# Second half of the gate/up weights: from one step of four loads to four steps of one load, with a newly searched order of all steps

## The chip, the cores and the metric

The kernel runs on one core of one Trainium2 chip. A time is the device time of one execution in microseconds (us). Three runs of the kernel before gave 573.64, 573.01 and 571.33 us, median 573.01. One more execution was taken with the profiler; it is the source of all durations below.

The engines are called by their names or by the short names of the profile: TensorE (PE, with its weight loads PEld), VectorE (DVE), ScalarE (ACT), GpSimd (POOL) and SyncE (SP). SP computes nothing here; it issues all plain transfers. GpSimd issues the gathers.

## The reference

Four sequences of 512 tokens, 256 features. Each goes through attention (16 heads of 16, causal, with a bias that falls with distance), a residual and a layernorm, and then through a mixture of 64 experts of which each token takes 8, with a shared expert beside them, a residual and a second layernorm:

```python
q, k, v = x @ Wq, x @ Wk, x @ Wv                       # (4, 512, 256), 16 heads
w = softmax((where(causal, q @ k.T, NEG) + slope * (j - i)) / sqrt(16))
x = layernorm(x + (w @ v) @ Wo + bo)
topv, topi = top_k(x @ gate_w.T, 8);  rw = softmax(topv)
gate, up = split(einsum('nh,eih->nei', x, gu_w))       # 64 experts, 64 + 64 wide
out = einsum('nei,ehi->nh', silu(gate) * up * W, dp_w) # W: rw at the chosen experts, else 0
out = out + sigmoid(x @ sh_gate1_w.T) * shared_expert(x)
return layernorm(x + out)
```

The kernel doesn't compute every expert for every token. It sorts the tokens of an expert into slots, runs each expert on its slots alone, writes the results to a table in DRAM (`rows_out`) and gathers for each token the eight rows that belong to it.

## The kernel before, in words

**Strands and letters.** The work is written as twelve generators ("strands"), each of which yields after a step. The string `ORDER` has one letter for each step, 851 in all; the loop at the end of the kernel takes the letters one after the other and advances the strand of that letter by one step. Every engine runs its instructions in the order in which the steps emit them, and so does SP's queue of transfers. Nothing is reordered at run time: the string alone decides what stands behind what. It was found by a search that is not part of the kernel. The strands:

- `p` project: transposes a batch and computes its q, k and v (lines 600 to 634)
- `s` scores: q times k on TensorE (L653), the exponential on ScalarE (L658), the causal mask on GpSimd (L663)
- `v` context: probabilities times v (L681), the transpose and division (L694 to L706), and at the end of a batch the output projection `po` (L715) and the sum with x (L719)
- `r` route: first layernorm, gate logits, the top 8, the slots (`code`), the rows to gather (`at`) and the weights `w8`; its `pick` products run on VectorE (L808) and GpSimd (L811), and its reductions on VectorE (L813)
- `t` turn: closes the memory of the attention and opens the pool `late` in its place
- `h` prepare: splits x into three bf16 parts, builds the one-hot tile `hot`, and runs the second layer of the shared expert (`sd`, L849, L854)
- `g` gather: for a group of 16 experts, brings the tokens into slots by matmuls with `hot` (`px`, L879); ScalarE and VectorE copy the result to `xt` (L869). Two letters a tile, four tiles a group: six matmuls a letter
- `u` up: two letters for a group of four experts ("quad"). The first issues the load of the quad's down weights `dq` (L897, 256 KB, three buffers), the second runs the gate/up matmuls (`gu`, L907) and the activation `ma` (ACT L914, DVE L915, L916)
- `d` down: the down matmuls (`y`, L927), ScalarE's copy `yq` (L932, two buffers), and the transfer of the rows to `rows_out` (L934, SP)
- `i` fetch: one gather of 128 rows from `rows_out` (L945, GpSimd), with five buffers `got`; a batch has 32 of them, and they need all rows of the batch
- `c` combine: VectorE adds a gathered tile with its weight to x (L956); after every 16 of them the second layernorm and the transfer of the output (L963)
- `z` check_range: a flag that tells whether the numbers kept within the range of this path; each engine then loads the flag into a register (L987), which its last branch uses

**Order of the batches.** The attention of the four batches comes first, with routing and slots of earlier batches among it. Then come 16 quads for each batch, and the gathers and combines of a batch among the quads of the next. What remains after the last quad is the gathers and combines of the last batch.

**The gate/up weights.** They are 8 MB, in eight chunks of 1 MB (`gu_sb`, tags `gu0` to `gu7`). One chunk serves two quads, so that quad q reads chunk q // 2, in every batch. Chunks 0 to 3 are loaded at the start of the kernel into memory of their own. Chunks 4 to 7 lie in the pool `late`, in memory that the attention has used. They can only be loaded when its last instruction, the output projection of batch 3, is done. The helper that loads them (L493) is

```python
for c in part:
    g_t = pool.tile([P, GUC, KC, 2, P], FP, tag=f"gu{c}", name=f"gu_sb{c}")
    nc.sync.dma_start(out=g_t, in_=gu[:, c * GUC : (c + 1) * GUC])
    gu_sb.append(g_t)
```

The `dq` buffers lie in the same pool.

Of the kernel before, what the change touches and what calls it, by code (L numbers as in the profile page):

```python
# [28 lines left out]
PRB = (2, 1, 1)  # L29

ORDER = (
    "pppppsppspsvsvsvsppvspppvvvsvsvvsvpspsvvvsvpsvvsvvrrsrpvvvsvsrhsrvrvvsrvssrrrrprvvsvhhhphpsprgsvhvgv"
    "rvsvrsvhhgsvgvrvvrvsvsrvsvvrpprsprsgvrrsrvvsvsgvvvhvrrsprpvrsgvsgrpvsrvpvrvrrsvsvsvvvrsvrssrvrrvsvsv"
    "rrrvvvvvvrvtrugugguuduggruuggrdgruugdugugrduurdguguduuggdggrgdgugguuuggdghuuhrhdhhuuhgduhuhdggudgugr"
    "uuggdgugdruggudgurrudguiirrhuuiiggdgccuguiridggicicucrudgiiguuciduggudcigciciccugurdgcgcucudgiguiiug"
    "gghhdhuuhduggghhudghhcuuduhgcduucuiggdguicugiidccigcdiuguciciuucciggduccigcugiidigccciiuguidciggciuu"
    "ggdcicicugugcccdiuugducuiciggggcgiggcghcdhuudichuuhiicidcihccuciuduuiccgghcgduuhhdgiuugiiidcicuggcud"
    "uggudccicigcdcigicuuuuccgcgiiidcigccucguiidiguuccicducugcdiugcugdgicciguiiuggcidcgiucgcuccidiuiudici"
    "guucccigdgiguiudcicciiugcgugidcidccuuccuiucdiciuuccdciiuidcihcicdicrczczcciicciiiiicccccccicicicicic"
    "iiiiciciciciciciciccccicicicicicicicicicciciccccccc"  # L40
)


# [360 lines left out]
def kernel(  # L404
# [26 lines left out]
    NP = NE // 2  # L431
    GUC = 4
# [21 lines left out]
    def single(name):  # L454
        return ps_s.tile([P, S], FP, tag="s", name=name)
# [34 lines left out]
    def load_gu(pool, part):  # L490
# [4 lines that stand above are left out]
# [61 lines left out]
    def transpose_in(src, b, what, pool, tag, bufs=1):  # L556

        dst = pool.tile([P, KC, S], FP, tag=tag, name=f"{what}_{b}", bufs=bufs)
        for c in range(KC):
            pt = single(f"pt_{what}_{b}_{c}")  # L560
            for t in range(NT):
                nc.tensor.transpose(pt[:, t * P : (t + 1) * P], src[:, t, c * P : (c + 1) * P], ident)
            if c:
                nc.vector.tensor_copy(dst[:, c, :], pt)
            else:
                nc.scalar.copy(dst[:, c, :], pt)  # L566
        return dst
# [29 lines left out]
    qTs, kTs, cxs, probs, late = {}, {}, {}, {}, {}  # L597

    def project():

        for b in range(B):
            xb = xs[b]
            xT = transpose_in(xb, b, "xT", apool, "xT", 2)
            nc.gpsimd.tensor_tensor(xb, xb, bo_b[:, None, :].to_broadcast([P, NT, E]), ALU.add)
            yield
            qT = qTs[b] = apool.tile([P, KC, 2, S], FP, tag="qT", name=f"qT_{b}", bufs=2)
            kT = kTs[b] = apool.tile([P, KC, S], FP, tag="kT", name=f"kT_{b}", bufs=2)
            for c in range(KC):
                for n in "qk":
                    ps = single(f"p{n}_{b}_{c}")  # L610
                    for kc in range(KC):
                        nc.tensor.matmul(  # L612
                            ps, w_sb[n][:, kc, c * P : (c + 1) * P], xT[:, kc, :],
                            start=(kc == 0), stop=(kc == KC - 1),
                        )
                    if n == "k":
                        nc.scalar.copy(kT[:, c, :], ps)
                    else:
                        for par in range(2):
                            nc.vector.tensor_scalar(qT[:, c, par, :], ps, own[:, par : par + 1], None, ALU.mult)  # L620
                    yield
            for t in range(0, NT, 2):
                pv = single(f"pv_{b}_{t}").rearrange("p (t h d) -> p t h d", h=HEADS, d=HD)
                for u in range(2):
                    for kc in range(KC):
                        nc.tensor.matmul(  # L626
                            pv[:, u], xT[:, kc, (t + u) * P : (t + u + 1) * P], w_sb["v"][:, kc, :],
                            start=(kc == 0), stop=(kc == KC - 1),
                        )
                for u in range(2):  # L630
                    nc.vector.tensor_tensor(
                        vas[b % 2][:, t + u, :, 0:HD], pv[:, u],
                        decay[:, t + u, :, None].to_broadcast([P, HEADS, HD]), ALU.mult,
                    )
                yield
# [5 lines left out]
    def scores():  # L641

        for b in range(B):
            for c, par, n in units:
                widths = [S - kb * P for kb in blocks[n]]
                pr = apool.tile([P, 4, sum(widths)], FP, tag=f"pr{n}", name=f"pr_{b}_{c}_{par}_{n}", bufs=PRB[n])
                probs[b, c, par, n] = pr
                s_ps = [double(f"sT_{b}_{c}_{par}_{n}_{i}") for i in range(2)]
                for m, kb in enumerate(blocks[n]):
                    lo = sum(widths[:m])  # L650
                    for r in range(4):
                        rows = slice(32 * r, 32 * r + 32)
                        nc.tensor.matmul(  # L653
                            s_ps[r // 2][:, r % 2, lo : lo + widths[m]], kTs[b][rows, c, kb * P : (kb + 1) * P],
                            qTs[b][rows, c, par, kb * P :], start=True, stop=True, skip_group_check=True,
                        )
                for i in range(2):
                    nc.scalar.activation(  # L658
                        pr[:, 2 * i : 2 * i + 2, :], s_ps[i][:, :, : sum(widths)], AF.Exp, scale=1.0 / HD**0.5
                    )  # L660
                for m in range(len(widths)):
                    lo = sum(widths[:m])
                    nc.gpsimd.affine_select(  # L663
                        out=pr[:, :, lo : lo + P], in_=pr[:, :, lo : lo + P], pattern=[[0, 4], [1, P]],
                        compare_op=ALU.is_ge, fill=0.0, base=0, channel_multiplier=-1,
                    )
                yield
# [157 lines left out]
    def prepare():  # L825

        for b in range(B):
            parts[b] = [mpool.tile([P, NT, E], BF, tag=f"x{n}", name=f"x{n}_{b}") for n in "hml"]
            for t in range(NT):
                h, m, l = (p[:, t, :] for p in parts[b][:3])  # L830
                xb = xs[b][:, t, :]
                left = mpool.tile([P, E], FP, tag="left", name=f"left_{b}_{t}")
                nc.scalar.copy(h, xb)
                nc.vector.tensor_tensor(left, xb, h, ALU.subtract)
                nc.scalar.copy(m, left)
                nc.vector.tensor_tensor(l, left, m, ALU.subtract)
                yield
                o = mpool.tile([P, WIDTH, NE], BF, tag=f"hot{t}", name=f"hot_{b}_{t}")
                nc.vector.tensor_tensor(
                    o, codes[b][:, t, None, :].to_broadcast([P, WIDTH, NE]), window, ALU.is_equal  # L840
                )
                parts[b].append(o)
                yield

            sa, sig = shares[b]
            sd = double(f"sd_{b}").rearrange("p j (t e) -> p (j t) e", e=E)
            for t in (0, 2, 1, 3):
                i = t // 2
                nc.tensor.matmul(  # L849
                    sd[:, t, :], sa[64 * i : 64 * i + 64, (t % 2) * P : (t % 2 + 1) * P],  # L850
                    shdp_sb[64 * i : 64 * i + 64, :], start=True, stop=True,
                )
            for t in range(NT):
                nc.vector.scalar_tensor_tensor(  # L854
                    xs[b][:, t, :], sd[:, t, :], sig[:, t, :], xs[b][:, t, :], ALU.mult, ALU.add
                )
            yield
# [110 lines left out]
    def turn():  # L968

        early.close()  # L970
        late["pool"] = fast.enter_context(tc.tile_pool(name="late", bufs=1))
        load_gu(late["pool"], range(NP // GUC // 2, NP // GUC))
        yield

    def check_range():

# [11 lines left out]
        yield  # L988

    strands = dict(  # L990
        p=project(), s=scores(), v=context(), r=route(), t=turn(), h=prepare(), g=gather(), u=up(), d=down(),
        i=fetch(), c=combine(), z=check_range(),
    )
    with tc.manual_schedule():
# [64 lines left out]
```

## Time and profile before

| what | value |
|---|---|
| median of three runs | 573.01 us |
| profiled execution | 531.3 us |
| its span, first to last instruction | 529.5 us |
| mean granted clock of TensorE | 0.936 |
| TensorE busy | 437.3 us, 83% |
| VectorE busy | 336.6 us, 64% |
| ScalarE busy | 246.1 us, 46% |
| GpSimd busy | 210.3 us, 40% |
| moved by DMA | 82.10 MB, mean 155 GB/s |

The profile is of one execution; this one took 531.3 us, of which 1.8 lie outside the span. A row of the list of instructions gives the start, the length, the engine, the line, the operation with "output <- inputs", the shape, and in brackets how long the engine stood idle before it and what ended this. "SPq" is SP issuing a transfer: the length is that of issuing, not of moving data. In the table of stretches a row gives the stretch, its length, the busy time of PE, PEld, DVE, ACT and POOL, the granted clock, the busy share of the DMA engines and GB/s.

### The profile page before, as it was taken

The numbers are of one execution on the slowest core, as the hardware profiler recorded it, in microseconds if no ns is written. First come the engines' busy times: TensorE is split into PE (matmuls) and PEld (weight loads), VectorE is DVE, ScalarE is ACT, GpSimd is POOL, SyncE is SP. The second block draws the span as 40 slices with busy tenths as digits, with TensorE's granted clock in tenths as the row PEclk, the third lists the DMA queues.
The fourth block names the chain that finished last, engine by engine and source line by source line (L and its number), as shares of the span: only waits on it lengthen the run. The fifth ranks groups of instructions, "written<-read, shape, count | busy, mean of one in ns | idle before, by whom it ended". The sixth has DMA issues, their size and how long they took to land.

```text
span 529.5 us, 12357 instructions
## 1 busy us (share of the span) xinstructions
PE 437.3 (83%) x4873; PEld 298.9 (56%) x4873; DVE 336.6 (64%) x944; ACT 246.1 (46%) x446; POOL 210.3 (40%) x233
## 2 busy tenths in 40 slices
PE   4999999999999986799999999999999899800000
PEld 2545455555446545587877777876778777700000
DVE  2312467786767664364777888778877687765633
ACT  1374657565553751355655556555655455400000
POOL 7051413433233231000004670174564657567770
PEclk9999999999999999799999999999999999975555
DMA  8800000000000006565555886696888889953331
GB/s 245 344 1 1 2 1 1 2 1 1 1 1 1 2 2 256 188 232 181 181 204 195 280 278 229 239 309 213 289 294 277 289 297 318 302 180 111 118 101 33
DMA packets 31907, 82.10 MB, mean 155 GB/s; under 512 B 4704, under 2 KB 10336, under 8 KB 30816
## 3 DMA queue, kind: packets, MB, share of 16 engines
q1 hardware_dynamic: 25696, 64.44, 34.3%
q0 software_dynamic: 6144, 16.79, 10.8%
q8 instruction: 40, 0.66, 0.6%
q14 instruction: 27, 0.22, 0.1%
HBM read 45.55 MB, written 35.65 MB: 153 GB/s over the span
## 4 chain that ended last, share of the span: by engine, by line
PE 51%; DMA 17%; issue 15%; DVE 6%; POOL 5%; ACT 3%; SPq 1%; POOLq 0%; DVEq 0%; ACTq 0%
DMA got<-rows_out,at 13%; PE gu L907 9%; PE sT L653 9%; PE av L681 6%; PE px L879 5%; PE y L927 5%; POOL got L945 5%; PE pq L612 3%; PE pk L612 3%; DMA dq<-in_dp_dram 3%; PE pv L626 3%; PE po L715 3%; ACT pr L658 2%; DVE x L956 2%; PE pt_c L694 2%
## 5 line engine op out<-in xcount | busy, mean ns | idle before, releaser
L945 POOL DMA_INDIRECT got<-rows_out,at x128 | 132.3, 1033 | 152.8 <-DVE x L956 66.1
L907 PE MATMUL gu<-xt,gu_sb 128*64 128x128 f32 x2048 | 125.7, 276 | 0.0
L907 PEld LDWEIGHTS gu<-xt,gu_sb 128*64 128x64 f32 x2048 | 110.9, 137 | 18.5 <-issue 17.1
L658 ACT ACTIVATE pr<-sT 128x768 f32<-128x768 f32 (+1 forms) x96 | 79.1, 881 | 43.2 <-PE sT L653 43.2
L956 DVE SCALAR_TENSOR_TENSOR x<-got,w,x 128x256 f32<-128x256 f32 x128 | 63.0, 494 | 42.1 <-DMA got<-rows_out,at 40.8
L932 ACT COPY yq<-y 128x1024 f32<-128x1024 f32 x64 | 64.8, 1012 | 45.1 <-PE y L927 41.0
L663 POOL TENSOR_SCALAR_AFFINE_SELECT pr<-pr 128x512 f32<-128x512 f32 x64 | 40.9, 651 | 106.4 <-ACT pr L658 105.2
L927 PE MATMUL y<-dq,ma 64*128 64x256 f32 x512 | 69.4, 390 | 10.7 <-DMA dq<-in_dp_dram 9.3
L869 DVE COPY xt<-px 128x512 f32<-128x512 f32 x64 | 43.7, 684 | 25.9 <-ACT xt L869 25.3
L927 PEld LDWEIGHTS y<-dq,ma 64*128 64x128 f32 x512 | 46.1, 189 | 19.6 <-issue 12.4
L869 ACT COPY xt<-px 128x192 f32<-128x192 f32 (+1 forms) x128 | 46.4, 376 | 20.2 <-PE px L879 15.8
L653 PE MATMUL sT<-qT,kT 32*128 32x256 f32 (+3 forms) x512 | 54.0, 467 | 0.3 <-ACT pr L658 0.2
L914 ACT ACTIVATE ma<-gu 128x256 f32<-128x256 f32 x64 | 24.6, 384 | 55.1 <-PE gu L907 55.1
L879 PE MATMUL px<-hot,xh 64*128 64x320 bf16 x256 | 39.6, 303 | 5.3 <-ACT xt L869 3.3
L915 DVE SCALAR_TENSOR_TENSOR ma<-ma,gu 128x256 f32<-128x256 f32 x64 | 26.6, 416 | 22.1 <-ACT ma L914 21.9
L681 PE MATMUL av<-pr,va 128*32 128x128 f32 (+3 forms) x512 | 40.4, 438 | 0.3 <-ACT xT L566 0.3
L879 PE MATMUL px<-hot,xl 64*128 64x320 bf16 x256 | 39.1, 299 | 0.0
L879 PE MATMUL px<-hot,xm 64*128 64x320 bf16 x256 | 39.0, 299 | 0.0
L811 POOL TENSOR_TENSOR pick<-pick,rest 128x512 f32<-128x512 f32 x16 | 20.8, 1302 | 42.1 <-DVE pick L808 35.5
L653 PEld LDWEIGHTS sT<-qT,kT 32*128 32x128 f32 x512 | 25.1, 183 | 18.7 <-issue 12.8
L916 DVE TENSOR_TENSOR ma<-gu,ma 128x256 f32<-128x256 f32 x64 | 27.1, 424 | 2.2
L681 PEld LDWEIGHTS av<-pr,va 128*32 128x32 f32 x512 | 13.7, 109 | 25.8 <-issue 18.1
(116 smaller groups left out, 483.2 us busy)
## 6 DMA issues: line engine op xcount, KB each, us to landing
rows_out<-yq SPq DMA_DIRECT2D x64, 512.0 KB, 4.2
dq<-in_dp_dram SPq DMA_DIRECT2D x64, 256.0 KB, 4.5
gu_sb<-in_gu_dram SPq DMA_DIRECT2D x8, 1024.0 KB, 8.9
x<-in_x_dram SPq DMA_DIRECT2D x4, 512.0 KB, 6.2
got<-rows_out,at POOLq DMA_INDIRECT x128, 3.7
out_dram<-x SPq DMA_DIRECT2D x8, 256.0 KB, 3.3
wq_sb<-in_wq_dram SPq DMA_DIRECT2D x1, 256.0 KB
wk_sb<-in_wk_dram SPq DMA_DIRECT2D x1, 256.0 KB
```

Of the source, the lines that this page charges most:

```text
L612: nc.tensor.matmul(ps, w_sb[n][:, kc, c * P : (c + 1) * P], xT[:, kc, :], start=(kc == 0), stop=(kc == KC - 1),)
L653: nc.tensor.matmul(s_ps[r // 2][:, r % 2, lo : lo + widths[m]], kTs[b][rows, c, kb * P : (kb + 1) * P], qTs[b][rows, c, par, kb * P :], st ...
L658: nc.scalar.activation(pr[:, 2 * i : 2 * i + 2, :], s_ps[i][:, :, : sum(widths)], AF.Exp, scale=1.0 / HD**0.5)
L663: nc.gpsimd.affine_select(out=pr[:, :, lo : lo + P], in_=pr[:, :, lo : lo + P], pattern=[[0, 4], [1, P]], compare_op=ALU.is_ge, fill=0.0, ...
L681: nc.tensor.matmul(av[32 * r : 32 * r + 32, kb * P :], vas[b % 2][:, kb, 8 * c + 2 * r + par, :], pr[:, r, lo : lo + w], start=(kb == 0), ...
L869: copy(xt[:, kc, :, t * CELL + lo : t * CELL + hi], ps[:, kc, lo * GROUP : hi * GROUP].rearrange("p (s e) -> p e s", e=GROUP),)
L879: nc.tensor.matmul(ps[:, kc, first : first + WIDTH * GROUP], parts[b][i][PART * half : PART * half + PART, t, kc * P : (kc + 1) * P], o[PA ...
L907: nc.tensor.matmul(gu_ps[64 * e : 64 * e + 64, j, which, :], gu_sb[p // GUC][:, p % GUC, kc, which, 64 * e : 64 * e + 64], xt[:, kc, QUAD ...
L927: nc.tensor.matmul(ys[:, e, j, :], a[64 * e : 64 * e + 64, j, :], dq[64 * e : 64 * e + 64, j, :], start=True, stop=True,)
L932: nc.scalar.copy(yq.rearrange("s j e h -> s e j h"), ys)
L945: nc.gpsimd.indirect_dma_start(out=g, out_offset=None, in_=rows_out[b], in_offset=bass.IndirectOffsetOnAxis(ap=ats[b][:, t, k : k + 1], ax ...
L956: nc.vector.scalar_tensor_tensor(acc[:, t, :], got.pop(n), w8s[b][:, t, k : k + 1], acc[:, t, :], ALU.mult, ALU.add)
```

## The change

The step `t` no longer loads chunks 4 to 7. A new strand `l` (`rest_of_up`) loads one of them at each of its four steps. The string has four letters more, and all of it is new: another search was run with the new letter, so that nearly every step from the first scores steps on stands at another place. Apart from the places, the same steps are taken: the numbers of `p`, `s`, `v`, `r`, `h`, `g`, `u`, `d`, `i`, `c` and `z` are unchanged.

```diff
@@ ORDER (cut to the lines around the turn) @@
-    "rrrvvvvvvrvtrugugguuduggruuggrdgruugdugugrduurdguguduuggdggrgdgugguuuggdghuuhrhdhhuuhgduhuhdggudgugr"
...
+    "vhrvvvvvrgvrvtgggrruuugguugllldrruguduuggggrgdguuduggurrddguuugudgguluggduggghuhduuhdhhuhugduuggdhud"
...
@@ turn @@
         early.close()
         late["pool"] = fast.enter_context(tc.tile_pool(name="late", bufs=1))
-        load_gu(late["pool"], range(NP // GUC // 2, NP // GUC))
         yield
+
+    def rest_of_up():
+
+        for c in range(NP // GUC // 2, NP // GUC):
+            load_gu(late["pool"], [c])
+            yield
@@ strands @@
-        p=project(), s=scores(), v=context(), r=route(), t=turn(), h=prepare(), g=gather(), u=up(), d=down(),
+        p=project(), s=scores(), v=context(), r=route(), t=turn(), l=rest_of_up(), h=prepare(), g=gather(), u=up(), d=down(),
         i=fetch(), c=combine(), z=check_range(),
```

What SP issues around the turn, in the order of its queue:

| before | after |
|---|---|
| chunk 4, 5, 6, 7 | dq_0, dq_1, dq_2 |
| dq_0, dq_1 | chunk 4, 5, 6 |
| rows_out of y_0 | rows_out of y_0 |
| dq_2, dq_3 | dq_3 |
| rows_out of y_1 | rows_out of y_1 |
| dq_4 ... | dq_4 ..., and chunk 7 between rows_out of y_6 and dq_9 |

Other places that move: the projections of batch 1 (`p`) come together ahead of the first context steps of batch 0. TensorE has six groups of px and two of gu between `po` and y_0, where it had three and two. Before the last down step 94 gathers are issued instead of 93, and the last two gathers of batch 2 and the first one of batch 3 stand ahead of the register load of `z` in GpSimd's queue, where all three stood behind it.

More of the change, by code (lines that the diff above doesn't have):

```diff
@@ L31 @@
 ORDER = (
-    "pppppsppspsvsvsvsppvspppvvvsvsvvsvpspsvvvsvpsvvsvvrrsrpvvvsvsrhsrvrvvsrvssrrrrprvvsvhhhphpsprgsvhvgv"
-    "rvsvrsvhhgsvgvrvvrvsvsrvsvvrpprsprsgvrrsrvvsvsgvvvhvrrsprpvrsgvsgrpvsrvpvrvrrsvsvsvvvrsvrssrvrrvsvsv"
-    "rrrvvvvvvrvtrugugguuduggruuggrdgruugdugugrduurdguguduuggdggrgdgugguuuggdghuuhrhdhhuuhgduhuhdggudgugr"
[L35 to L40, printed above, removed]
+    "pppppsppspsppppsppvvvsvsvsvvspsvvsvvsvspvsvvsvsvsvvrvvsvsrrvsvvvrhsvrrsvvsrhrsvrsprrphprppshvvvvrgpg"
+    "vsvrsvhvpsrvvrrvrsvsvsvvsrsvhhvrsvvsprvsvvhrsrvrsvvgrrpprgvrpsrvgpsvrrrvrsvsvvsvvgrsrrsvvvvrrsrssrrg"
+    "vhrvvvvvrgvrvtgggrruuugguugllldrruguduuggggrgdguuduggurrddguuugudgguluggduggghuhduuhdhhuhugduuggdhud"
+    "gughugugdrgugdruudugguughidriiigdggcruuccgiuiicciigdggruccicuuiidiggcuuiggccrdiguucccdiugudgrgcuuiig"
+    "gcdcugigghhudhuuhdughudghhuuhgduugcgduuiicggdcigcucigiudggciciccuuicggdguuiicdigchcdicuicuiguciuggdc"
+    "cciuiudicccguggucicdcgugiccuiidigiuugdccciggicuiuigggcrgidghcuuhdhhuuduhicchgicucdugigiduhuugghcdugu"
+    "gdgcuugdcicuuicggiccciduiuiccicidgigugcgiucgidcuicgucciidgcuiugdccgcuiiugdcccgiucgicdgicuugudcgcigcu"
+    "iiggiuccciduiuiigccdicugcuccidiguiuicduudcccuciciuducuidiccuiihcidrcciicdiicizzcicicicicccccciiciicc"
+    "iciicicicicicicicciiciccccicicicicicicicicicicicccccccc"
 )
```

## The prediction

> **What bounds the kernel now.** I read the engine totals first, then the slices, then the wait that stands out in them, and last the end of the span. Engine totals and slices of the page of before (a digit is tenths of a slice of 13.2 us):
>
> ```profile
> PE 437.3 (83%) x4873; PEld 298.9 (56%) x4873; DVE 336.6 (64%) x944; ACT 246.1 (46%) x446; POOL 210.3 (40%) x233
> ...
> PE   4999999999999986799999999999999899800000
> ...
> PEclk9999999999999999799999999999999999975555
> DMA  8800000000000006565555886696888889953331
> ```
>
> (In the third line the digits begin right after the name; it is the granted clock of TensorE.) TensorE is full from slice 2 to about slice 35, with one notch at slices 16 and 17, and has nothing to do in the last five. So there are two stretches with different limits: TensorE sets the time up to its last expert step at 465 us, and after that a tail of 64.5 us runs through the gathers of the last batch. A hole in TensorE's line before 465 us is time of the kernel, one for one.
>
> The notch in the list of TensorE's instructions, and what SyncE (SP) issued then (start, length, both us; in brackets the idle time before):
>
> ```profile
> 205.38 1.97 PE L907 MATMUL gu<-xt,gu_sb 128*64 128x128 f32 x32
> 215.29 2.08 PE L927 MATMUL y<-dq,ma 64*128 64x256 f32 x8 [7.95 <-DMA dq<-in_dp_dram]
> ...
> 221.89 1.03 PE L927 MATMUL y<-dq,ma 64*128 64x256 f32 x8
> ```
>
> ```profile
> 202.26 2.07 SPq L493 DMA_DIRECT2D gu_sb<-in_gu_dram  x4
> 204.38 0.97 SPq L897 DMA_DIRECT2D dq<-in_dp_dram  x2
> 218.45 0.33 SPq L934 DMA_DIRECT2D rows_out<-yq  x1
> ```
>
> The first down step y_0 wants its weights dq_0 (256 KB) at 207.3. They were issued at 204.4, behind four 1 MB loads of gate/up weights in the same queue, and came at 215.2: 10.8 us, where the DMA issues give a median of 4.5 us for dq. The stretches around it show why: 430 GB/s from 208 to 212, all engines full, and the clock at 0.58 and 0.56 from 212 to 220.
>
> ```profile
> 208.00:212.00 4.00, 0.00 (x0) 0.00 (x0) 0.66 (x2) 0.00 (x0) 0.00 (x0) 1.00 1.02 430
> 212.00:216.00 4.00, 0.70 (x4) 0.68 (x6) 0.00 (x0) 0.00 (x0) 0.00 (x0) 0.58 0.77 313
> 216.00:220.00 4.00, 4.00 (x36) 2.79 (x34) 1.22 (x3) 1.66 (x3) 0.00 (x0) 0.56 0.20 80
> ```
>
> Start of the tail (GpSimd's list):
>
> ```profile
> 466.99 0.99 POOL L945 DMA_INDIRECT got<-rows_out,at  x1 [0.30 <-DVE w L813]
> 470.42 0.99 POOL L945 DMA_INDIRECT got<-rows_out,at  x1 [2.43 <-DVE x L956]
> 471.71 0.99 POOL L945 DMA_INDIRECT got<-rows_out,at  x1 [0.30 <-issue]
> 473.01 1.00 POOL L945 DMA_INDIRECT got<-rows_out,at  x1 [0.30 <-issue]
> ```
>
> The last 34 gathers run from 470.42 to 515.24 at a pitch of 1.30 us. Counted back from the end, 470.42 and 471.71 belong to batch 2, and 473.01 is the first of batch 3.
>
> **The Trainium skill.** "DMA: Bandwidth & Descriptors", section "Queues, rings and completion order", says that an SDMA engine takes the descriptors of one ring in ring order. The trace agrees: dq_0 came only after the 4.2 MB ahead of it. "TensorE: Matmul & The Clock Gate", Part 1, says that after an idle window of about 3.4 us TensorE runs at half clock until it has been busy about as long. The trace agrees: after 7.95 us of idling y took 2.08 us instead of 1.03.
>
> **The change, part by part.** The same instructions run in both kernels. What changes is the order, which the two instruction lists show.
>
> *Removed: four gate/up loads ahead of dq_0.* SP now issues dq_0, dq_1, dq_2, then three of the loads, and the fourth between dq_8 and dq_9. What goes: 7.95 us of idling, and the slow clock after it: y 2.08 - 1.03 = 1.05; twelve px 1.60 for 0.92 (chain), 0.68; gu 2.16 for 1.90, 0.26. Sum 9.95 us.
>
> *Does the wait go elsewhere?* Count from P, the end of the last output projection po (202.05 in before), when SP is released, as memory of the attention comes free; dq_0 now carries this wait. dq_0 issued at P+0.2 lands at P+4.7 (4.5 median) to P+5.3 (5.1 in this stretch). TensorE has before y_0: six px groups of 0.46, two gu of 1.90: P+6.6. VectorE has before ma_0 (from P+0.9): xt 0.68, w 0.68, three small ones 0.56, statistics 1.76, then ma 0.85: P+5.4. So no wait at y_0, by a margin of 1.2 us.
> Behind it, the three loads: 3 x 1.05 + 3 x 0.26 = 3.93 MB at 430 GB/s are 9.1 us, so from P+1.0 they fill the queue to about P+10. The first rows_out is issued at P+8.9 (y_0 to P+7.6, copy 1.0) and lands at about P+13.5 rather than P+13.1. It holds up yq_2, which is due at P+17: from y_0 to y_2 TensorE has gu 1.9, px 0.5, y 1.0, gu 1.9, px 1.8, transposes 1.0, px 0.5. dq_3, issued after it (SP is in order), lands at about P+14.5; y_3 comes at P+19.5. Nothing waits, with 3.5 us and 5 us in hand. Chunks 4 to 6 are first read by gate/up step 8, chunk 7 by step 14, each over 20 us of TensorE work after its load; the fourth load delays dq_9 and one rows_out by 1.05 MB / 430 GB/s = 2.4 us, with 3 dq buffers and 9 us from issue to use. Cost 0; without this cover 2.4 us.
>
> *Moved: the rest of the order.* Attention: TensorE idles 4.1 us in 10 to 200 (190 less 39.7, 49.5, 49.0, 47.7). In the new order batch 1 is projected right after batch 0. Between a scores step and the context step that reads it lie under 2.5 us of TensorE work in 4 cases (3 before); the exp of 2 x 0.88 and the mask of 0.65 need that. Taken 0, from -2 to +3 us, as no row shows this order.
> Expert steps: I put TensorE's 1.90, 0.96 and 0.46 us on the letters. Between a gather and its combine lie under 3 us in 17 cases of the first 92, before in 10. A gather takes 1.0 and lands 3.7 later, so VectorE waits there, and behind it stand xt copies and ma. In before such waits sum to 17.6 us up to 463 us, and TensorE lost 3.2 us through VectorE (1.7, 0.2, 1.3). Times 17/10: 2.2 us lost. Adjacent px halves (0.41 each) are 7 instead of 8: -0.4. Net +1.8, from 0 to +5.
> Tail: in before, the range check's register load (0.53 us, issued 469.0) stands in GpSimd's queue ahead of the last two gathers of batch 2, which so start 1.4 us after the flag. In the new order these two are ahead, and batch 3's first gather stands ahead of the load. It can start when the last rows_out has landed: last y ends at 464.96, issue 466.13, landing 4.0: 470.1 instead of 473.01. The load then costs 0.5 to 1.4 between the first and second gather; the 0.5 us by which layernorm held up a gather at 480.06 goes. Gain 2.0 to 2.9, taken 2.4.
>
> Sum: -9.95 + 1.8 - 2.4 = -10.55. Of the profiled 531.3 us (span 529.5) 520.7 are left. The median of the runs, 573.01, is 42 us above this execution, and nothing in the profile says where they lie; I take the same microseconds off: 562.4. Scaled by 573/531 it would be 561.6.
>
> **Rivals.** *The wait comes back three steps later* (yq_2 on rows_out, y_3 on dq_3). Against it stand 3.5 and 5 us of margin at 430 GB/s. If the loads ran at only 178 GB/s (what moved from 215 to 260, where nothing pressed), 3.93 MB took 22 us and dq_3 came at P+24.5: 5 us of hole and up to 1.5 us of slow clock. Gain 4: 569.
> *No gain in the runs.* The 42 us would be a limit on TensorE's work over time, and the hole merely rest. Against it: clock 1.00 in nearly all full stretches. 573.
> *Slower: the combines.* Seven more short gaps times up to 2.7 us (4.7 less 2) are 19 us of VectorE standing still between 300 and 465 us. If all of it reached TensorE, 573.0 - 12.35 + 19 = 580. It decides from 15 us on; before passed on 3.2 of 17.6. That speaks against it, but TensorE has only two PSUM buffers for gate/up to run ahead.
> *More gain*: the runs have a longer hole than the profile (slower transfers), worth 16 us: 557 or less.
>
> **How the numbers follow.** Forecast as worked out 0.72 (own range 557 to 567), back later 0.10, no gain 0.05, slower 0.08, more 0.05. 0.5%, about what a measurement of this kernel can tell, is 2.9 us: 570.1 to 575.9. Faster: 0.72 + 0.10 + 0.05 less 0.02 at the edge = 0.85; same 0.07; slower 0.08. The range 555 to 569 leaves out slower and no gain, the upper half of "back later", and the far end of "more": under 0.2.
>
> **What would show it.** Right: no idle over 1 us before the first y, no clock dip near 215, dq_0 landing in about 5 us, last y about 8 us earlier, batch 3's first gather about 5 us after it. Wrong: an idle time at y_3 or yq copies <- rows_out (the return), VectorE's waits for got well over 30 us ahead of the last y with px waiting for xt (the slower rival), or a new idle time over 3 us of TensorE in the attention.

## The result, and the profile after

| runs | before, us (runs) | changed, us (runs) | ratio, 95% interval | difference |
|---|---|---|---|---|
| the comparison that the forecast was made for | 572.33 (4) | 565.60 (4) | 0.9887 [0.9849, 0.9925] | -6.7 us |
| both kernels again, chip A | 572.48 (18) | 566.91 (6) | 0.9911 [0.9887, 0.9935] | -5.6 us |
| both kernels, chip C | 530.54 (11) | 518.03 (5) | 0.9756 [0.9740, 0.9773] | -12.5 us |

One of the 18 runs of before on chip A took 1524 us and is left out of the ratio. The change makes the kernel faster by 1.1%; the forecast was 562.4 us, 1.85% under 573.01. The table also shows where the 42 us lie between the profile of before (531.3 us) and its timed runs (573 us), which the forecast had left open. They go with the chip. The experiments ran on four, called A to D here: before takes 572 us on A and 531.3, 530.5 and 531.7 us on B, C and D. The profile that the forecast read is like B, C and D. The times that it had to forecast are like A, and so is the first profile of the changed kernel, of an execution of 567.88 us. Engine totals and slices of its page (a slice is 14.1 us):

```profile
PE 453.8 (80%) x4873; PEld 308.8 (55%) x4873; DVE 337.2 (60%) x944; ACT 245.5 (43%) x446; POOL 210.1 (37%) x233
...
PE   4999999999999899999879799978997876930000
...
PEclk9999999999999999999998899997999989885555
```

The notch at slices 16 and 17 is gone. But from slice 20 on TensorE has small holes and dips of its clock, and its 4873 matmuls are busy for 16.5 us longer than in the profile of before. On chip C the same kernel shows none of that (a slice is 12.9 us):

```profile
PE 433.7 (84%) x4873; PEld 295.7 (57%) x4873; DVE 340.4 (66%) x944; ACT 246.2 (48%) x446; POOL 209.4 (40%) x233
...
PE   4999999999999999999999999999999998810000
...
PEclk9999999999999999999999999999999999965555
```

TensorE is full from slice 2 to slice 33, with no notch and no dip of the clock before the tail. The mechanism of the forecast is therefore read on chip C, against the profile of before, which is of the same kind. TensorE's instructions around y_0, then SP's (start, length, in us; `...` stands for rows that are cut, here and below):

```profile
204.34 1.97 PE L907 MATMUL gu<-xt,gu_sb 128*64 128x128 f32 x32
...
206.66 1.03 PE L927 MATMUL y<-dq,ma 64*128 64x256 f32 x8
207.62 1.97 PE L907 MATMUL gu<-xt,gu_sb 128*64 128x128 f32 x32
...
209.93 1.03 PE L927 MATMUL y<-dq,ma 64*128 64x256 f32 x8
```

```profile
199.70 1.28 SPq L897 DMA_DIRECT2D dq<-in_dp_dram  x3
201.02 1.38 SPq L493 DMA_DIRECT2D gu_sb<-in_gu_dram  x3
208.78 0.33 SPq L934 DMA_DIRECT2D rows_out<-yq  x1
209.22 0.36 SPq L897 DMA_DIRECT2D dq<-in_dp_dram  x1
```

y_0 starts with no idle time in brackets, 7.1 us after the last output projection (13.2 in before), and takes 1.03 us instead of 2.08. Of the three dq loads, now first in the queue, dq_1 lands 3.0 us after its issue and dq_2 5.7 us; the landing of dq_0 is not on record. dq_3, issued behind the three gate/up loads at 209.2, takes 6.8 us. The table of stretches (columns as before: length, PE, PEld, DVE, ACT, POOL, clock, DMA share, GB/s) shows that the DMA engines are full again, while TensorE works on:

```profile
204.00:208.00 4.00, 4.00 (x60) 3.10 (x57) 3.74 (x13) 1.80 (x5) 0.00 (x0) 1.00 0.94 337
208.00:212.00 4.00, 4.00 (x64) 3.37 (x62) 3.58 (x18) 2.44 (x4) 0.00 (x0) 1.00 1.00 411
212.00:216.00 4.00, 3.53 (x48) 2.61 (x44) 2.79 (x6) 2.02 (x7) 0.00 (x0) 1.00 0.97 383
```

From 208 to 212 they move 411 GB/s and TensorE is busy for all of the 4 us; in before it was busy for 0.00 us of the stretch with 430 GB/s.

The span in three parts, from the instruction lists (P is the end of the last output projection, E the start of the copy of the last y, both in us from the start of the span):

| stretch | before (profile on record) | changed, chip C | difference | forecast |
|---|---|---|---|---|
| start to P | 202.1 | 199.6 | -2.5 | 0 |
| P to E | 263.0 | 254.7 | -8.3 | -9.95 + 1.8 = -8.15 |
| E to the end | 64.4 | 63.2 | -1.2 | -2.4 |
| span | 529.5 | 517.5 | -12.0 | -10.55 |

### The profile page after: what moved, and what is told of

Its sections match the earlier page's. It is cut to its first block, busy times and chain, and to the rows that moved or that the text cites. A ratio compares the mean times of both kernels' runs of the same rounds, so it can differ in the third digit from the quotient of the medians.

```text
span 565.9 us, 12367 instructions
## 1 busy us (share of the span) xinstructions
PE 453.8 (80%) x4873; PEld 308.8 (55%) x4873; DVE 337.2 (60%) x944; ACT 245.5 (43%) x446; POOL 210.1 (37%) x233
## 4 chain that ended last, share of the span: by engine, by line
PE 71%; issue 7%; ACT 6%; another core or an unknown queue 5%; DVE 4%; DMA 4%; POOL 1%; POOLq 0%; SPq 0%; ACTq 0%; DVEq 0%
PE gu L907 21%; PE px L879 11%; PE y L927 10%; PE sT L653 7%; PE av L681 6%; PE pq L612 3%; PE po L715 3%; PE pk L612 3%; PE pv L626 3%; DMA got<-rows_out,at 2%; ACT pr L658 2%; PE pt_c L694 2%; ACT xt L869 2%; PE pl L736 1%
## 5 line engine op out<-in xcount | busy, mean ns | idle before, releaser
L907 PE MATMUL gu<-xt,gu_sb 128*64 128x128 f32 x2048 | 136.2, 286 | 4.0 <-issue 3.9
L907 PEld LDWEIGHTS gu<-xt,gu_sb 128*64 128x64 f32 x2048 | 118.6, 143 | 25.5 <-issue 24.4
L927 PE MATMUL y<-dq,ma 64*128 64x256 f32 x512 | 72.7, 398 | 0.3 <-issue 0.2
L879 PE MATMUL px<-hot,xh 64*128 64x320 bf16 x256 | 40.8, 309 | 28.2 <-ACT xt L869 25.3
L869 ACT COPY xt<-px 128x192 f32<-128x192 f32 (+1 forms) x128 | 46.4, 375 | 26.0 <-PE px L879 17.8
L927 PEld LDWEIGHTS y<-dq,ma 64*128 64x128 f32 x512 | 48.3, 194 | 9.7 <-issue 4.5
L653 PE MATMUL sT<-qT,kT 32*128 32x128 f32 (+3 forms) x512 | 51.8, 467 | 0.5 <-ACT pr L658 0.5
L879 PE MATMUL px<-hot,xl 64*128 64x320 bf16 x256 | 41.0, 305 | 1.5 <-issue 1.5
L879 PE MATMUL px<-hot,xm 64*128 64x320 bf16 x256 | 40.5, 304 | 2.0 <-issue 2.0
L879 PEld LDWEIGHTS <-xh 64*128 64x128 bf16 x256 | 14.5, 95 | 46.1 <-issue 43.8
```

The source lines that it names most:

```text
L653: nc.tensor.matmul(s_ps[r // 2][:, r % 2, lo : lo + widths[m]], kTs[b][rows, c, kb * P : (kb + 1) * P], qTs[b][rows, c, par, kb * P :], st ...
L869: copy(xt[:, kc, :, t * CELL + lo : t * CELL + hi], ps[:, kc, lo * GROUP : hi * GROUP].rearrange("p (s e) -> p e s", e=GROUP),)
L879: nc.tensor.matmul(ps[:, kc, first : first + WIDTH * GROUP], parts[b][i][PART * half : PART * half + PART, t, kc * P : (kc + 1) * P], o[PA ...
L907: nc.tensor.matmul(gu_ps[64 * e : 64 * e + 64, j, which, :], gu_sb[p // GUC][:, p % GUC, kc, which, 64 * e : 64 * e + 64], xt[:, kc, QUAD ...
L927: nc.tensor.matmul(ys[:, e, j, :], a[64 * e : 64 * e + 64, j, :], dq[64 * e : 64 * e + 64, j, :], start=True, stop=True,)
```

## The experiments

All were run beside the kernel before on the same chip. The first four ran on chip B, the next three on C, the next four on A, the last on D.

**The kernel before again.** No edit.

> The kernel before, unchanged, once more with the profiler, since its first profiled execution (531.3 us) was 40 us shorter than its timed runs and the changed kernel's (567.9 us) was not. If the 531.3 us were an exception: about 572 us, with TensorE standing still for 3 to 6 us about ten times after the gathers begin (about 280 us), as in the changed kernel's profile. If the profiler shortens this kernel's execution: about 531 us again. The last output projection po should end near 202 us and the first y should start near 215 us, after about 8 us without its weights, in either case.

531.76 us, and the same timeline: P at 202.5, first copy at 218.4, after 8.6 us in which y_0 waited for dq_0. So the profile on record was no exception among executions, and the profiler doesn't shorten anything: all 34 timed runs of before on chip B lie between 529.0 and 534.2 us.

**The loads alone, in the old order.**

```diff
 source of the changed kernel; ORDER of before, with the letters l put in
-    ...vtrugugguuduggruug...
+    ...vtrugugguudulllggruug...      and the fourth l ahead of the tenth dq load
```

> The old order, with only the four loads moved: three behind the third dq load, the fourth ahead of the tenth. Theory (the hole is the gain, 9.95 us by the forecast's sum): 562 to 563 us, ratio 0.983, no idle time of TensorE ahead of the first y. Rival (the gain comes from the new order of the other steps): 572 us. Rival (loads only shift the wait to the yq copies or a later y): 568 us and an idle time over 2 us at y_2 or y_3.

528.36 us against 531.33 (ratio 0.9936, 0.9917 to 0.9955): -3.0 us, near the third of these (-4 on the scale of 572). y_0 waits for nothing, but y_3 does. TensorE's list, with y_2 and y_3:

```profile
215.29 1.03 PE L927 MATMUL y<-dq,ma 64*128 64x256 f32 x8
...
223.03 2.08 PE L927 MATMUL y<-dq,ma 64*128 64x256 f32 x8 [3.90 <-DMA dq<-in_dp_dram]
```

And SP's:

```profile
201.99 0.80 SPq L897 DMA_DIRECT2D dq<-in_dp_dram  x2
209.22 0.33 SPq L934 DMA_DIRECT2D rows_out<-yq  x1
209.59 0.43 SPq L897 DMA_DIRECT2D dq<-in_dp_dram  x1
210.07 1.80 SPq L493 DMA_DIRECT2D gu_sb<-in_gu_dram  x3
211.99 0.36 SPq L897 DMA_DIRECT2D dq<-in_dp_dram  x1
```

This is the forecast's rival "the wait comes back", at the place that it named. In this order the step d_0 stands ahead of the third dq load. SP is in order, so rows_out of y_0, which waits for the copy of y_0, held dq_2 and the three loads behind it until 209.2. The loads went out at P + 8.2, in the changed kernel at P + 1.5. So dq_3 was issued right behind three of these loads and came 11.0 us later, and the y behind the wait ran at half speed (2.08 us).

**The order alone.** The changed kernel's ORDER without its letters l, and the four loads back in the step t, ahead of dq_0.

```diff
-    ...vtgggrruuugguugllldrr...
+    ...vtgggrruuugguugdrr...          and load_gu(... range(NP // GUC // 2, NP // GUC)) in turn()
```

> The new order of all other steps, but the four loads back in the step t, ahead of dq_0. Theory: the new order gives next to nothing by itself (forecast -0.6), but has 2.6 us more TensorE work ahead of the first y, so a hole of about 6 us and 2 us of slow clock come back: about 8 us over the changed kernel, 573 to 574 us. Rival (the gain comes from the order): 566 us, as the changed kernel.

530.14 us against 531.33 (0.9989, 0.9973 to 1.0005): no difference that can be told. The hole is back:

```profile
213.57 2.08 PE L927 MATMUL y<-dq,ma 64*128 64x256 f32 x8 [7.41 <-DMA dq<-in_dp_dram]
```

So neither part has the gain by itself (-1.2 and -3.0 us; together -12.5 on chip C). The new order does shorten the attention: P comes at 198.9 us here, at 202.5 in before on this chip. But P to E takes 264.9 us instead of 262.8, so most of that is lost again while the hole stands. I had expected 6 us of hole, as TensorE has three more groups of px ahead of y_0; but dq_0, now issued together with two more, came 12.5 us after its issue (at 201.1) instead of 10.8.

**The range check moved back.**

```diff
 from the last d on
-    d iicizzcic ...
+    d zczciiiic ...
```

> The changed kernel with the range check put back ahead of the last two gathers of batch 2 and the first of batch 3, as in the kernel before. Theory (the tail step of the forecast): 2.4 us slower than the changed kernel, about 568 us. Rival (the tail is held by something else, such as the last rows_out or the combines of batch 2): no difference, 565.6 us.

521.12 us on chip B, 0.9799 (0.9770 to 0.9827) of before. Without the changed kernel on the same chip this does not tell what the step is worth; the pair on chip A below does.

**The changed kernel on the same chip as before.** No edit.

> The changed kernel, unchanged, beside the kernel before on the same chip. The runs so far suggest that one chip takes about 531 us for the kernel before (the profiled execution of before, and all experiments so far) and another about 572 us (the timed runs and the profile of the changed kernel). Theory: where before takes 531 us, the changed kernel takes 521 to 522 us, ratio 0.981, as the forecast's sum against the profile had it, and TensorE has none of the dozen stalls of 3 to 6 us. Rival: the gain is 1.1% on every chip, 525.5 us. The tail step of the forecast would make it 2.4 us faster than the kernel with the range check moved back (521.1 us), 518.7 us; from that kernel's profile I now expect no gain there, because the fifth gather after batch 3's first one waits for a got buffer in place of it.

518.03 us, 0.9756 of before: better than the 521 to 522 that I expected. The stalls of the first profile are absent, so the rival of 1.1% on every chip falls. The number lies near what the forecast's tail step asked for here (518.7). That would have been the wrong reason, as the pair on chip A shows.

**Loads one by one, in the old order.**

```diff
-    ...vtrugugguuduggruuggrdgruugdugugrduurd...
+    ...vtrugugguuduggruulggrdgruulgdugulgrduulrd...
```

An l stands behind each letter that issues dq_3, dq_4, dq_5 and dq_6.

> The old order with the four loads placed one by one behind the loads dq_3, dq_4, dq_5 and dq_6, where three in a row behind dq_2 had brought a wait of 3.9 us at y_3. Theory: the hole is the gain and the order of the other steps matters little: no idle time over 1 us up to y_8, 521 to 522 us where before takes 531. Rival (the new order itself is worth several us): 525 us or more.

525.98 us against 530.54 (0.9907, 0.9884 to 0.9929): -4.6 us, the rival's number. y_3 no longer waits for weights. But now each of the next four rows_out stands behind a gate/up load in the queue, and ScalarE's copies, with two yq buffers, wait for rows_out to land. ScalarE's list:

```profile
225.77 1.01 ACT L932 COPY yq<-y 128x1024 f32<-128x1024 f32 x1 [3.09 <-DMA rows_out<-yq]
...
230.13 1.01 ACT L932 COPY yq<-y 128x1024 f32<-128x1024 f32 x1 [2.53 <-DMA rows_out<-yq]
...
234.51 1.01 ACT L932 COPY yq<-y 128x1024 f32<-128x1024 f32 x1 [2.54 <-DMA rows_out<-yq]
```

From P to the copy of y_3 this kernel needs 19.0 us (before 28.3), but from there to y_7 16.5 (before 13.5): 3 of the 9.3 us are given back. Beside the changed kernel its span is 6.6 us longer (524.1 us against 517.5): 2.6 us of that lie ahead of P, 2.4 between P and E, 1.6 in the tail. So when the loads go out one by one, most of what is left lies outside the stretch that the loads touch. Whether the old order would keep the whole gain with the three loads right behind dq_1, ahead of the first rows_out, was not run.

**Eight buffers for gathered rows.**

```diff
-RING = 5
+RING = 8
```

> The changed kernel with eight buffers for gathered rows instead of five. Theory (the tail is held up where the sixth gather of batch 3 waits for a buffer that stands behind batch 2's layernorm on VectorE): this wait of 1.8 us (3.1 us pitch instead of 1.3) and a smaller one of 0.5 us later go, 2 us faster than the changed kernel, about 519.5 us. Rival (the tail is set by 1.3 us a gather and by the last rows_out): the same as the changed kernel.

510.24 us on chip C, 0.9614 (0.9598 to 0.9631) of before and 7.8 us under the changed kernel, where I expected 2. The tail gave 3.0 us (E to the end 60.1 us instead of 63.2), but the larger part came before the last y: P to E took 248.9 us instead of 254.7. GpSimd's list around E (449.5 us):

```profile
447.25 1.00 POOL L945 DMA_INDIRECT got<-rows_out,at  x1 [0.31 <-issue]
448.55 1.00 POOL L945 DMA_INDIRECT got<-rows_out,at  x1 [0.30 <-DVE x L956]
454.72 1.00 POOL L945 DMA_INDIRECT got<-rows_out,at  x1 [5.17 <-DVE x L956]
```

All of batch 2 is gathered before the last y has left PSUM, and batch 3's first gather starts at E + 5.2, 4.2 us after the issue of the last rows_out (450.5). The row names VectorE, but the combine that frees its buffer lay eight gathers back. The likelier releaser is the landing of rows_out, which took 4.0 us in the median of the changed kernel's profile and so falls at about E + 5. TensorE's waits between 200 and 450 us fall to two rows, 3.8 us, with none for VectorE. This is the fastest version that was run.

**The changed kernel and the range check, both on chip A.** Kernels as above.

> The changed kernel again, to have it on one chip with the kernel that has the range check moved back. Where before takes 531 us: 518 us again. Where before takes 572 us: 565.6 us again, with TensorE's signals coming 1 to 6 us late about a dozen times.

> The changed kernel with the range check moved back, again, now on the same chip as the changed kernel. In the two profiles so far the tail itself, counted from the last y, differs by only 0.3 us (63.5 against 63.2), and 2.7 us lie before the last y, where both kernels issue the same instructions. Theory A (the 2.7 us came from the other chip; the range check costs what the tails show): 0.3 us slower than the changed kernel, same. Theory B (the forecast's step: 2.4 us): 2 to 3 us slower than the changed kernel on the same chip too.

566.91 and 566.97 us, ratios to before 0.9911 (0.9887 to 0.9935) and 0.9890 (0.9867 to 0.9914). Theory A holds: moving the range check is worth nothing that can be measured. The 2.7 us that lay before the last y between chips B and C (P to E 257.5 and 254.7 us) were not its doing. So chips that are alike in before can differ by 2 to 3 us in the changed kernel.

**Eight buffers in the kernel before, chip A.**

```diff
-RING = 5
+RING = 8
```

> The kernel before with eight buffers for gathered rows. If the five buffers cost what they cost the changed kernel (7.8 us): about 523 us where before takes 531 us. If the new order is what makes the buffers short: less than 3 us gained, 528 us or more.

575.70 us against 572.48 (1.0067, 1.0038 to 1.0096): slower by 0.7%. Neither of my two numbers covers that, both being worked out from a chip of the other kind. On chip A, letting gathers run ahead brought nothing.

**The kernel before with a profile, chip A.**

> The kernel before, for a profile on the same chip as the changed kernel. About 531 us or about 572 us, as the chip is; in the second case with the late signals of TensorE in it too. Its TensorE idles 7 to 8 us ahead of the first y in either case.

572.05 us. The profiles of chip A show what this document calls late signals: an instruction that waits for TensorE starts some us after TensorE's recorded end. The matmuls are the same, in the same order, on chip A and on chip B. From the list of all engines, chip A:

```profile
361.96 1.97 PE L907 MATMUL gu<-xt,gu_sb 128*64 128x128 f32 x32
...
364.61 1.05 POOL L945 DMA_INDIRECT got<-rows_out,at  x1 [0.30 <-issue]
...
365.10 0.47 PE L927 MATMUL y<-dq,ma 64*128 64x256 f32 x1 [0.45 <-issue]
...
366.50 0.94 PE L927 MATMUL y<-dq,ma 64*128 64x256 f32 x3 [0.93 <-issue]
...
367.26 0.99 POOL L945 DMA_INDIRECT got<-rows_out,at  x1 [0.30 <-issue]
367.94 1.24 PE L927 MATMUL y<-dq,ma 64*128 64x256 f32 x4 [0.50 <-issue]
...
368.56 1.00 POOL L945 DMA_INDIRECT got<-rows_out,at  x1 [0.30 <-issue]
...
370.92 0.38 ACT L914 ACTIVATE ma<-gu 128x256 f32<-128x256 f32 x1 [7.85 <-remote]
```

And chip B:

```profile
351.91 1.97 PE L907 MATMUL gu<-xt,gu_sb 128*64 128x128 f32 x32
...
353.92 0.38 ACT L914 ACTIVATE ma<-gu 128x256 f32<-128x256 f32 x1 [0.91 <-PE gu L907]
...
354.22 1.03 PE L927 MATMUL y<-dq,ma 64*128 64x256 f32 x8
```

On B ma starts 0.04 us after the last matmul of gu has ended, and the eight matmuls of y run in one piece. On A ma starts 7.0 us after it, and y comes in three pieces, each after an idle time that ends with "issue". The waits say it in one row, "ACT ma <- remote" (the profile finds no releaser), which the profiles of B, C and D do not have at all. Chip A, before:

```profile
ACT ma L914 <- remote: 32.4, 7, 7.9
```

For each of the 64 quads, take the time by which ma starts later than both the last gu matmul's end and the end of ScalarE's previous instruction. On A this is over 0.6 us in 18 quads of before, 44.9 us in all, and in 15 and 13 quads of the changed kernel's two profiles of this kind (42.7 and 37.1 us). On B and C it is at most 0.05 us in any quad. On A it goes with the gathers. In before, the 24 quads with no gather issued in the 5.5 us ahead of ma have a mean of 0.03 us, the 20 with three a mean of 1.93 us and up to 6.99 (on B 0.01).

**All gathers behind the last y.**

```diff
 ORDER of the changed kernel up to the last d
-    every i and c where it stands
+    without i and c; all of them, in the same sequence, behind the last d
```

> The changed kernel with all gathers and combines of batches 0 to 2 taken out of the expert steps and put behind the last y, in their old sequence. All the work is done, but the tail holds 128 gathers, so the whole takes some 630 us; the quantity is the stretch from the last output projection to the last y, which is 254.7 us in the changed kernel on a chip where it takes 518 us, and 297.6 us on the chip where it takes 567 us. Theory (on that chip TensorE's signals come late because of the gathers): about 247 us on either chip, no wait over 1.2 us between gu and ma. Rival (that chip delays TensorE's signals whenever other transfers run, gathers or not): well over 270 us there. On the other chips: 247 us, 5 to 8 less than now, would be what waiting combines on VectorE cost TensorE; unchanged 254 us would say that the combines cost TensorE nothing.

The whole took 629.94 us on chip D, where before takes 531.7. P to E is 246.7 us, and ma is nowhere over 0.05 us late. TensorE's only row of waits from 200 to 450 us:

```profile
PE px L879 <- ACT xt L869: 2.5, 6, 0.5
```

Against the 254.7 us of the changed kernel on C, the gathers and combines cost TensorE 8.0 us in its stretch, on chips without late signals. As D is not of A's kind, the run says nothing on whether the late signals of A would go with the gathers.

## Why the prediction was right, and where it was not

**The removed hole: right.** y_0 without a wait, at full clock, at P + 7.1 where P + 6.6 was forecast. From P to the copy of y_15 before takes 76.4 us and the changed kernel 67.3 on C, 9.1 less, though three more groups of px (1.4 us by the forecast's own 0.46 us) now lie behind P. -9.95 + 1.4 is -8.6. (The parts of the hole add up to 9.94.)

**No return of the wait: right for this placement, and narrower than the forecast made it.** y_2, y_3 and the copies do not wait on C, though with less in hand than worked out: dq_3 landed at about P + 16.4, not P + 14.5, and y_3 came at P + 20.3. But the two runs with the old order lost by just the two ways named: dq behind the loads (P to the copy of y_3 took 23.4 us with three loads in a row, 19.0 with single ones), and copies behind rows_out (3 us up to y_7). By these runs the changed kernel owes its gain not to the margin alone, but to SP having issued the three loads by 202.4, before it has to wait for the first rows_out. The two runs differ from it in the order of the other steps too; the old order with the loads at that place was not run.

**Attention: at the edge of its range.** Taken 0 from -2 to +3; measured -2.5 between these two profiles, and -3.0 as a mean over the profiles (P at 202.1 in six with the old order, at 199.1 in the eight with the new, chips of both kinds among them). 1.4 us of it are the px groups moved behind P, which the sum did not book as moved. Where the other 1.6 us come from stays open.

**Expert steps, +1.8: right in sum by luck.** P to E is -8.3 for a forecast of -8.15. Its ingredient was not: VectorE's waits for got up to E rose from 15.2 us (before, chip B; 17.8 in the profile that the forecast read) to 18.4 us (C), not by 17/10. By the run with the gathers behind the last y TensorE loses to gathers and combines not the 3.2 us read from its rows of waits but about 8. Before loses about the same by this reckoning (263.0 - 9.95 = 253.05 us of P to E without its hole, against 246.7 - 1.4 = 245.3 without gathers, 7.8), so the error cancelled. The rival "slower through the combines" falls with it.

**Tail, -2.4: this step failed.** Measured -1.2 on C. The forecast took an earlier first gather of batch 3 for an equally earlier end. On C (GpSimd's list; three of batch 2, the last of them at 459.63, then batch 3's first):

```profile
456.91 1.12 POOL L945 DMA_INDIRECT got<-rows_out,at  x1 [0.65 <-DVE x L956]
458.33 1.00 POOL L945 DMA_INDIRECT got<-rows_out,at  x1 [0.30 <-DVE x L956]
459.63 1.00 POOL L945 DMA_INDIRECT got<-rows_out,at  x1 [0.31 <-issue]
460.94 1.00 POOL L945 DMA_INDIRECT got<-rows_out,at  x1 [0.30 <-DVE x L956]
```

At E + 6.6 GpSimd has only just come through batch 2's gathers, the first of which here waited 0.65 us for VectorE to free a buffer. The last rows_out, issued by 455.7 and with 3.6 us to landing by the answer for its line, was there at about E + 5. So the first gather comes 1.3 us earlier (before E + 7.9), not 2.9, and the sixth gather of batch 3 then waits for a buffer for longer than in before (a pitch of 2.2 us instead of 1.8). With the check moved back the first gather does come later on A, at E + 8.0 instead of E + 6.6. But the sixth starts at E + 15.0 against E + 14.9, the tail is 64.6 us against 64.5, and the times are equal. What the register load costs at the first gather is lost in any case at the sixth, where the five buffers are used up. The forecast's pitch of 1.30 us has no such waits in it; over its own 34 gathers the mean is 1.36.

**From the profile's sum to the runs: the term that failed.** "I take the same microseconds off" gave 562.4. On chips of the profile's kind 518.0 was measured for a sum of 520.7. On the chip of the times, 6.7 and 5.6 us were measured for 10.55. That this still lies in the range is in part luck: nothing in the working stood for what chip A takes back. Progress from P shows where the rest went:

| from P to | before, chip A | changed, chip A | difference | difference, chip C to B |
|---|---|---|---|---|
| copy of y_15 | 76.7 | 67.3 | -9.4 | -9.7 |
| copy of y_23 | 111.3 | 110.7 | -0.5 | -7.9 |
| copy of y_39 | 195.7 | 192.1 | -3.6 | -10.3 |
| copy of y_63 | 301.9 | 297.7 | -4.3 | -8.0 |

The column of the changed kernel on A is from its fastest execution there (563.3 us). In its first profile (567.9 us) y_23 comes at 111.8 and y_63 at 302.2, so that the differences are +0.5 and +0.3: after y_15 single executions on A differ by as much as the change is worth.

On A the hole's gain is whole at y_15, the last of these ahead of the first gather (271.4 us), and nearly gone eight quads later. There the changed kernel's ma is late by 3.5 us at quad 21, TensorE stands still behind it, and its next gu takes 3.68 us instead of 1.97:

```profile
295.61 0.45 PE L879 MATMUL px<-hot,xh 64*128 64x320 bf16 x2 [3.67 <-ACT xt L869]
...
296.52 3.68 PE L907 MATMUL gu<-xt,gu_sb 128*64 128x128 f32 x32
```

In before three quads up to there are late too (19, 21 and 22), but only by 1.2 to 1.3 us each. TensorE stands still for 1.4 us once, and no gu is slow; its 4.9 us come only at quad 25. Later the two take turns. So what failed is the transfer of the microseconds to the chip of the times. How much of them a new order keeps there seems to be set by how its gathers fall, not by the loads; that is read from these profiles and not tested. The profile of the fast kind could not show it. The range (555 to 569) held all the same, and the two rivals "no gain in the runs" (573) and "the wait comes back" (569) were not what happened.

## What to carry to other kernels

Of loads that share a queue with urgent ones, put the urgent ones first and the rest directly behind them, ahead of the first transfer that has to wait for a result: in the old order, with the same loads 7 us later and behind such a transfer, 3.0 us were gained of a hole of 9.95. A hole that is closed by moving loads can so come back in part at a later step; run the moved loads and the new order apart before crediting one. Where a profile's own time and the timed runs differ by far more than their spread, take a profile that agrees with the runs before using its microseconds.

## What the runs showed that was not expected

The same kernel takes 530 to 532 us on three chips and 572 us on the fourth, with equal timelines up to the gathers (P at 202.3 on A, 202.5 on B; first gather at 283.9 and 284.4 us). From the first gather to the last copy A takes 220.3 us and B 180.9: nearly the whole difference lies there. The Trainium skill, "Perfetto Trace Analysis", section "Tensor Engine Instruction (MATMUL, LD_WEIGHTS)", says that a matmul's recorded end is estimated and that its semaphore update follows only when PSUM has acknowledged the data. The lists of A fit with that, but the page gives no size, and here the recorded end of gu and the start of ma lie up to 7 us apart. Whether the matmuls themselves stood still, or their writes, or only the update, is open, and so is the reason why this chip does it. The traces have one more sign: of the DMA landing signals of before, 2798 are on record on A and 4517 on B, for the same transfers, and of the engines' own signals 4804 and 6666. In any 30 us there are at most 292 landing signals on A and up to 603 on B. With so many missing, the releaser that a row of A names ("remote", "issue") is weak evidence; the start times do not depend on it. Every run on record, timed ones too, lists a span and a granted clock, so whether the recording itself has a part in A's time is open as well. That the late signals come from the gathers is shown only as the two going together.

Three buffers more are worth 7.8 us to the changed kernel on C, most of it before the last y; the same edit in before costs 3.2 us on A. An edit that lets gathers run closer together can so have one sign on one chip and another on the next; that the kernels differ too keeps this from being shown.
